# Perceiver block on one core: the two slot streams change the order of their half passes

## The chip, the cores and the metric

The kernel runs on one core of a Trainium2 chip. A core has TensorE (PE, matmuls; its weight loads are listed as PEld), VectorE (DVE), ScalarE (ACT), GpSimd (POOL) and SyncE (SP, here only a DMA queue), and 16 DMA engines. The metric is device time in microseconds (us) of one execution, lower is better. The kernel before took 1061.83 us (median of 3 runs, 1057.53 to 1068.19).

## The reference

`x` has 8 batches of 64 slots of width 512, `ctx_1024` has 8 batches of 1601 rows of width 512, all float32. Three blocks follow each other, each added to `x`. The first is the one that the change is in:

```python
Pn = rmsnorm(P, input_norm_w); k_proj = Pn @ Wk.T; v_proj = Pn @ Wv.T     # P = ctx_1024
for _ in range(3):
    sn = rmsnorm(slots, slot_norm_w); q_proj = sn @ Wq.T
    scores = einsum('bkd,bmd->bkm', q_proj, k_proj) * SCALE
    attn = softmax(scores, axis=-2)                        # over the 64 slots
    attn = attn / (sum(attn, axis=-1, keepdims=True) + EPS)
    updates = einsum('bkm,bmd->bkd', attn, v_proj)
    slots = gru_cell(updates, slots, wih, whh, bih, bhh)   # gates r, z, n
```

Then come a 16-head self-attention over 64 positions, and a mixture of 8 experts (2 per row) with 2 shared experts.

## The kernel before

**Tiling.** The 8 batches are four pairs, t = 0 to 3; a pair is 128 slots on 128 partitions. Its context has 13 row tiles of 128 rows per batch (the last has 65). `k_proj` and `v_proj` are never formed: `Wq` and `Wk` are folded into `wqk`, and `Wv` and the input gates' weights into `wvi` (`fold_values`, three parts of 32 matmul instructions), so both products run against the raw context.

**One pass** (t, it) has two halves, which the code calls X and Y.

- X is `attend`: transpose the slots (`tr_s`, copied to `sT`), query `pq` = `sT` x `wqk`, copy it (`q`), transpose it (`tr_q`), scale it (`qT`), score it in four column groups (`sc`, lines 358 to 370: 64 matmul instructions per pass) against the transposed context, copy each group into `raw` (ACT); then the softmax in four chunks of up to four tiles: transposes `tr_e`, then reduce, subtract, multiply, Exp, sum, reciprocal, two multiplies on DVE and ACT (lines 395 to 402, result `e`), and the weighted sums `part` on POOL (lines 404 to 410). In the first pass of a pair X also makes the transposed context (`prepare`): 26 tiles are transposed (`tr_p`), copied to `pT_a` by DVE and ACT in turns, squared on ACT for the norm, and written to DRAM (`kept`), from where later passes load it (`pT_X`).
- Y is `update`: `pu` = `e` x raw context rows (52 matmul instructions, line 433), `rs` (line 440), the recurrent part of the gates `recur` (`pr`, `pz`, `phn` <- `whh`, `sT`: 8 instructions each), `upd` = `pu` scaled (DVE, then ACT), transpose (`tr_u`, copied to `uT`), the input part of the gates (`pr`, `pz`, `pxn` <- `wvi`, `uT`: 8 each), and lines 456 to 470, which make the new slots on DVE and ACT.

**Order of the halves.** Pairs 0 and 2 are one stream (`lead`, six passes), pairs 1 and 3 the other (`trail`). The list `stages` (lines 199 to 204) gives X(0,0) Y(0,0), and then four halves at a time: X trail, X lead, Y trail, Y lead. So two X follow each other, and then two Y: X(1,0) X(0,1) Y(1,0) Y(0,1), X(1,1) X(0,2) Y(1,1) Y(0,2), X(1,2) X(2,0) Y(1,2) Y(2,0), X(3,0) X(2,1) Y(3,0) Y(2,1), X(3,1) X(2,2) Y(3,1) Y(2,2), X(3,2), and Y(3,2) at line 723, behind the first two pairs' projections of the self-attention. The loop at lines 504 to 521 issues them.

**What sets the order on an engine.** The framework's planner orders the instructions when the program is built: where they stand in the program is their priority, and an instruction that is not ready by its reckoning lets a later one of the same engine pass. In the trace, recurrent matmuls of one stream stand between the scores of the other. On the chip every engine then works its list in order. DMAs that are issued through `queue` keep the program's order on SP. `pump` (line 242) puts them there: `plan` lists, by stage, which row chunks (`nat`, 5 buffers of 1 MB) and transposed groups (`ctxT`, 5 buffers) are wanted, and each `done` frees a buffer and lets the next load be issued.

**PSUM.** There are 8 banks, four of the tag `gate` and four of the tag `ring`. `gate` holds `pr`, `pz`, `phn`, `pxn`, and `tr_p` of `prepare`; `ring` holds everything else. The buffer tag `wide` (`raw` and `e`) has 3 buffers, `sT`, `quT` and `nat` of the work pool have 2 each.

Of the kernel before, what the change touches and what calls it, by code (L numbers as in the profile page):

```python
# [39 lines left out]
def perceiver_kernel(  # L40
# [155 lines left out]

    lead = [(t, it) for t in (0, 2) for it in range(ITERS)]
    trail = [(t, it) for t in (1, 3) for it in range(ITERS)]  # L200
    stages = [("X", lead[0]), ("Y", lead[0])]
    for n in range(len(trail)):
        both = trail[n : n + 1] + lead[n + 1 : n + 2]
        stages += [("X", u) for u in both] + [("Y", u) for u in both]

# [62 lines left out]
    def prepare(t):  # L270

        ss = small.tile([P, NMT, 2], F32, tag="pss", name=f"pss_{t}", bufs=4)
        nc.gpsimd.memset(ss, 0.0)
        for g, (lo, hi) in enumerate(GROUPS):
            for j in range(2):
                b = 2 * t + j
                key = plan["ctxT"].pop(0)[1]
                assert key == ("made", "X", t, 0, j, g)
                held["ctxT"] += 1
                ct = chunk(f"pT_{b}_{g}_a", "ctxT")[:, : DC * (hi - lo)]  # L280
                c3 = ct.rearrange("p (c m) -> p c m", c=DC)
                for i in range(lo // P, (hi + P - 1) // P):
                    src = row_tile("X", t, 0, j, i)
                    k = src.shape[0]
                    junk = work.tile([P, D], F32, tag="junk", name=f"junk_{b}_{i}")
                    nc.scalar.activation(  # L286
                        junk[:k], src, AF.Square, accum_out=ss[:k, i, j : j + 1]
                    )
                    evacuate(
                        c3[:, :, i * P - lo : i * P - lo + k],  # L290
                        transpose4(src, f"p_{b}_{i}", k, "gate"),
                    )
                    row_used(i)
                nc.gpsimd.dma_start(kept[b][g], ct)  # L294
                tiles[key] = c3
            yield g
        v = small.tile([P, NMT, 2], F32, tag="pv", name=f"pv_{t}", bufs=2)
        nc.vector.tensor_scalar(v, ss, 1.0 / D, 1e-6, ALU.mult, ALU.add)
        ri = const.tile([P, NMT, 2], F32, name=f"inv_{t}")
        flat = "p i j -> p (i j)"  # L300
        rsqrt(ri.rearrange(flat), v.rearrange(flat), 2 * NMT, f"p_{t}")
        rms = const.tile([P, NMT, 2], F32, name=f"rms_{t}")
        nc.vector.tensor_mul(rms, v, ri)
        inv_of[t], rms_of[t] = ri, rms
# [27 lines left out]

    slots_of, sT_of = {}, {}

    def attend(t, it, first=lambda g: None):

        n = f"{t}_{it}"
        slots = slots_of[t]
        sT = work.tile([P, DC, P], F32, tag="sT", name=f"sT_{n}", bufs=2)
        nc.vector.tensor_copy(sT, transpose4(slots, f"s_{n}"))  # L340
        sT_of[t] = sT
        ss = small.tile([P, 1], F32, tag="sss", name=f"sss_{n}")
        junk = work.tile([P, D], F32, tag="junk", name=f"junk_{n}")
        nc.scalar.activation(junk, slots, AF.Square, accum_out=ss)
        nc.vector.tensor_scalar(ss, ss, 1.0 / D, 1e-6, ALU.mult, ALU.add)
        ri = small.tile([P, 1], F32, tag="sri", name=f"sri_{n}")

        pq = bank(f"pq_{n}")
        matmul4(pq, lambda c: sT[:, c, :], lambda c: wqk[:, c, :])
        q = work.tile([P, D], F32, tag="nat", name=f"q_{n}", bufs=2)  # L350
        nc.scalar.copy(q, pq)
        rsqrt(ri, ss, 1, f"s_{n}")
        qT = work.tile([P, DC, P], F32, tag="quT", name=f"qT_{n}", bufs=2)
        nc.vector.tensor_mul(  # L354
            qT, transpose4(q, f"q_{n}"), qscale.unsqueeze(2).to_broadcast([P, DC, P])
        )
        raw = work.tile([P, NMT * P], F32, tag="wide", name=f"raw_{n}", bufs=3)
        for g, (lo, hi) in enumerate(GROUPS):
            first(g)
            sc = bank(f"sc_{n}_{g}")[:, : hi - lo]  # L360
            cols = [tiles[("col" if it else "made", "X", t, it, j, g)] for j in range(2)]
            for c in range(DC):
                for j in range(2):
                    nc.tensor.matmul(  # L364
                        sc[j * S : (j + 1) * S, :],
                        lhsT=qT[:, c, ts(j, S)], rhs=cols[j][:, c, :],
                        start=c == 0, stop=c == DC - 1,
                    )
            done("ctxT", 2)
            nc.scalar.mul(raw[:, lo:hi], sc, ri)  # L370

        e = work.tile([P, NMT * P], F32, tag="wide", name=f"e_{n}", bufs=3)
        mx = small.tile([P, 2 * NMT], F32, tag="mx", name=f"mx_{n}")
        sm = small.tile([P, 2 * NMT], F32, tag="sm", name=f"sm_{n}")
        inv = inv_of[t].rearrange("p i j -> p (i j)")
        rms = rms_of[t].rearrange("p i j -> p (i j)")

        part = work.tile([P, P], F32, tag="part", name=f"part_{n}", bufs=2)
        for lo in range(0, NMT, 4):
            hi = min(lo + 4, NMT)  # L380
            k = P if lo < MT else TAIL
            pt = bank(f"tr_e_{n}_{lo}")[:k, : (hi - lo) * P]
            for i in range(lo, hi):
                nc.tensor.transpose(pt[:, ts(i - lo, P)], raw[:, i * P : i * P + k], ident)  # L384
            r, w = slice(2 * lo, 2 * hi), 2 * (hi - lo)

            def rows3(v):
                return v.rearrange("p (r k) -> p r k", k=S)

            def wide(v):  # L390
                return v[:k, r].unsqueeze(2).to_broadcast([k, w, S])

            ee = rows3(e[:k, lo * P : hi * P])
            mxr, smr = mx[:k, r], sm[:k, r]
            nc.vector.reduce_max(mxr, rows3(pt), axis=AX.X)  # L395
            nc.vector.tensor_sub(ee, rows3(pt), wide(mx))
            nc.vector.tensor_mul(ee, ee, wide(inv))  # L397
            nc.scalar.activation(ee, ee, AF.Exp)  # L398
            nc.vector.reduce_sum(smr, ee, axis=AX.X)
            nc.vector.reciprocal(smr, smr)  # L400
            nc.vector.tensor_mul(smr, smr, inv[:k, r])
            nc.vector.tensor_mul(ee, ee, wide(sm))
            prod = raw[:k, lo * P : hi * P]
            nc.gpsimd.tensor_mul(rows3(prod), ee, wide(rms))  # L404
            if hi - lo > 1:
                nc.gpsimd.tensor_add(prod[:, : 2 * P], prod[:, : 2 * P], prod[:, 2 * P :])
                one = part if lo == 0 else prod[:, :P]
                nc.gpsimd.tensor_add(one, prod[:, :P], prod[:, P : 2 * P])
            if lo:
                nc.gpsimd.tensor_add(part[:k], part[:k], prod[:, :P])  # L410
        return e.rearrange("p (i k) -> p i k", k=P), part

    def recur(t, it):

        n = f"{t}_{it}"
        banks = [bank(f"{g}_{n}", "gate") for g in ("pr", "pz", "phn", "pxn")]
        for j, pg in enumerate(banks[:3]):
            matmul4(
                pg, lambda c: sT_of[t][:, c, :], lambda c: whh_s[j][:, c, :], stop=j == 2
            )  # L420
        return banks

    def update(t, it, att, banks=None):

        n = f"{t}_{it}"
        e, part = att
# [19 lines left out]
        upd = work.tile([P, D], F32, tag="nat", name=f"upd_{n}", bufs=2)  # L446
        nc.vector.tensor_scalar_mul(upd[:, :H], pu[:, :H], cs)
        nc.scalar.mul(upd[:, H:], pu[:, H:], cs)
        uT = work.tile([P, DC, P], F32, tag="quT", name=f"uT_{n}", bufs=2)
        nc.vector.tensor_copy(uT, transpose4(upd, f"u_{n}"))  # L450
        for j, pg in enumerate((pr, pz, pxn)):
            matmul4(
                pg, lambda c: uT[:, c, :], lambda c: wvi[j][:, c, :], start=j == 2
# [21 lines left out]


    wvi = [chunk3(f"wvi_{j}") for j in range(3)]
    whh_s = []

    def fold_values(j):  # L480
        for dc in range(DC):
# [7 lines left out]
    def start_group(g):  # L489
# [2 lines left out]
            return  # L492
        for n in (g, g + 1):
            next(columns)
            if g == 0:
                fold_values(n)
        if g == 0:
            whh_s.extend(load_w(whhT, j, f"whh_{j}", queue) for j in range(2))
        if g:
            for _ in columns:  # L500
                pass

    att = {}
    for pos, (half, (t, it)) in enumerate(stages[:-1]):
        if pos == 1:
            fold_values(2)
            whh_s.append(load_w(whhT, 2, "whh_2", queue))
        if half == "Y":
            update(t, it, att.pop(t))
            continue  # L510
        if it == 0:
            slots_of[t] = work.tile([P, D], F32, tag="slots", name=f"slots_{t}_0", bufs=4)
# [1 line left out]
            columns = prepare(t)  # L514
            if pos == 0:
                done("nat", 2)
                att[t] = attend(t, it, start_group)
                continue
            for _ in columns:
                pass  # L520
        att[t] = attend(t, it)

# [520 lines left out]
```

## Time and profile before

| | |
|---|---|
| median of 3 runs | 1061.83 us |
| the profiled execution | 1067.05 us, span 1065.3 us, mean granted TensorE clock 0.969 |
| PE busy | 971.7 us, 91% of the span, 4081 matmul instructions |
| DVE, ACT, POOL busy | 428.6, 246.7, 198.0 us |
| DMA | 237.41 MB, mean 223 GB/s |
| slot passes (102 to 783 us of the span) | PE busy 634.03 of 681 us, DMA 247 GB/s |
| what follows (783 to 1065 us) | PE busy 247.35 of 282 us |

The page's slices are 26.6 us each, with the busy share in tenths. Matmuls are pipelined and their ends are modelled, so "busy" is not a statement that the array does useful work at its peak; the idle time in front of a matmul, which the timeline puts in brackets with what ended it, is what an order can remove. A float32 matmul of 512 columns is two instructions; eight in a row take 3.43 to 3.70 us. In the timeline a row `x8` is eight instructions, and the first number is their start.

### The profile page before, as it was taken

The numbers are of one execution on the slowest core, as the hardware profiler recorded it, in microseconds if no ns is written. First come the engines' busy times: TensorE is split into PE (matmuls) and PEld (weight loads), VectorE is DVE, ScalarE is ACT, GpSimd is POOL, SyncE is SP. The second block draws the span as 40 slices with busy tenths as digits, with TensorE's granted clock in tenths as the row PEclk, the third lists the DMA queues.
The fourth block names the chain that finished last, engine by engine and source line by source line (L and its number), as shares of the span: only waits on it lengthen the run. The fifth ranks groups of instructions, "written<-read, shape, count | busy, mean of one in ns | idle before, by whom it ended". The sixth has DMA issues, their size and how long they took to land. (4 is left out here: it accounts for less than half of the span.)

```text
span 1065.3 us, 11266 instructions
## 1 busy us (share of the span) xinstructions
PE 971.7 (91%) x4081; PEld 461.3 (43%) x4081; DVE 428.6 (40%) x1059; ACT 246.7 (23%) x530; POOL 198.0 (19%) x295
## 2 busy tenths in 40 slices
PE   6899989899989997999898899899998988899994
PEld 3454354334433444444543344333443464675441
DVE  3224155532544347522554224452451445542223
ACT  1652552110211524205521001110110111211220
POOL 2003013300133004300132100330051211031221
PEclk9999999999999998999899999999999969999998
DMA  9946678864656647845787564596191300039943
GB/s 344 400 135 274 249 296 347 317 255 168 246 232 263 246 136 270 316 151 214 306 336 270 223 247 186 197 357 247 59 348 40 129 2 0 1 134 309 371 158 136
DMA packets 62425, 237.41 MB, mean 223 GB/s; under 512 B 5870, under 2 KB 20222, under 8 KB 50080
## 3 DMA queue, kind: packets, MB, share of 16 engines
q1 hardware_dynamic: 52576, 195.44, 48.6%
q0 software_dynamic: 8640, 39.14, 9.4%
q10 hardware_dynamic: 1152, 2.10, 0.5%
q8 instruction: 33, 0.54, 0.2%
q14 instruction: 24, 0.20, 0.0%
HBM read 201.22 MB, written 36.48 MB: 223 GB/s over the span
## 5 line engine op out<-in xcount | busy, mean ns | idle before, releaser
L433 PE MATMUL pu<-pn_Y,e 128*64 128x512 f32 x576 | 144.1, 609 | 5.7 <-DMA pn_Y<-in_ctxp 5.7
L364 PE MATMUL sc<-pT_X,qT 128*64 128x384 f32 (+1 forms) x512 | 102.4, 505 | 11.7 <-DMA pT_X<-kept 7.4
L404 POOL TENSOR_TENSOR raw<-e,rms 128x512 f32<-128x512 f32 (+1 forms) x48 | 44.8, 936 | 275.4 <-DVE sm L400 153.1
L433 PEld LDWEIGHTS pu<-pn_Y,e 128*64 128x64 f32 x576 | 42.3, 139 | 95.7 <-issue 79.6
L286 ACT ACTIVATE junk<-pn_X 128x512 f32<-128x512 f32 x96 | 60.4, 629 | 40.9 <-DMA pn_X<-in_ctxp 38.6
L364 PEld LDWEIGHTS sc<-pT_X,qT 128*64 128x64 f32 x512 | 38.1, 136 | 70.2 <-issue 47.8
L110 PE MATMUL tr_p<-ident,pn_X 128*128 128x128 f32 x384 | 53.4, 290 | 14.0 <-DMA pn_X<-in_ctxp 8.8
L395 DVE TENSOR_REDUCE mx<-tr_e 128x8 f32<-128x512 f32 (+1 forms) x48 | 26.9, 581 | 97.4 <-PE tr_e L384 97.3
L294 POOL DMA_DIRECT2D kept<-pT_a x32 | 17.4, 545 | 214.3 <-ACT r L467 66.3
L84 DVE COPY pT_a<-tr_p 128x512 f32<-128x512 f32 x52 | 34.7, 685 | 53.1 <-PE tr_p L110 31.8
L110 PEld LDWEIGHTS tr_p<-ident,pn_X 128*128 128x128 f32 x384 | 44.4, 147 | 26.9 <-issue 14.6
L370 ACT ACTIVATE raw<-sc,sri 128x384 f32<-128x384 f32 (+1 forms) x48 | 28.6, 596 | 107.8 <-PE sc L364 107.6
L153 PE MATMUL pq<-wqk,sT 128*128 128x512 f32 x96 | 48.0, 646 | 4.9 <-DVE sT L340 3.9
L153 PE MATMUL pr<-wvi,uT 128*128 128x512 f32 x96 | 45.5, 617 | 4.1 <-DVE uT L450 3.9
L398 ACT ACTIVATE e<-e 128x512 f32<-128x512 f32 (+1 forms) x48 | 25.8, 547 | 98.9 <-DVE e L397 98.8
L364 PE MATMUL sc<-pT_a,qT 128*64 128x384 f32 (+1 forms) x256 | 46.2, 503 | 2.4 <-DVE qT L354 2.4
L153 PE MATMUL pr<-whh,sT 128*128 128x512 f32 x96 | 48.1, 612 | 0.0
L153 PE MATMUL pqkv<-wqkv,haT 128*128 128x512 f32 x96 | 44.2, 618 | 1.4 <-ACT haT L549 1.4
L153 PE MATMUL pz<-whh,sT 128*128 128x512 f32 x96 | 44.7, 597 | 0.0
L153 PE MATMUL pab<-up_b,xT 128*128 128x512 f32 x96 | 43.2, 594 | 0.8 <-ACT xT L86 0.7
L153 PE MATMUL phn<-whh,sT 128*128 128x512 f32 x96 | 43.5, 592 | 0.0
L153 PE MATMUL pz<-wvi,uT 128*128 128x512 f32 x96 | 43.2, 592 | 0.0
(240 smaller groups left out, 1348.1 us busy)
## 6 DMA issues: line engine op xcount, KB each, us to landing
pn_Y<-in_ctxp SPq DMA_DIRECT2D x72, 1024.0 KB
pT_X<-kept SPq DMA_DIRECT2D x48, 768.0 KB
pn_X<-in_ctxp SPq DMA_DIRECT2D x24, 1024.0 KB
kept<-pT_a POOLq DMA_DIRECT2D x24, 768.0 KB, 8.6
pT_X<-kept SPq DMA_DIRECT2D x16, 898.0 KB
up_b<-in_w SPq DMA_DIRECT2D x24, 512.0 KB
kept<-pT_a POOLq DMA_DIRECT2D x8, 898.0 KB, 10.1
dn_b<-in_w SPq DMA_DIRECT2D x12, 512.0 KB
```

What stands on the lines that cost most here:

```text
L84: nc.vector.tensor_copy(dst, src)
L110: nc.tensor.transpose(pt[:, c, :rows], src[:rows, ts(c, P)], ident[:rows, :rows])
L153: nc.tensor.matmul(dst, lhsT=lhsT(c), rhs=rhs(c), start=start and c == 0, stop=stop and c == DC - 1,)
L286: nc.scalar.activation(junk[:k], src, AF.Square, accum_out=ss[:k, i, j : j + 1])
L294: nc.gpsimd.dma_start(kept[b][g], ct)
L364: nc.tensor.matmul(sc[j * S : (j + 1) * S, :], lhsT=qT[:, c, ts(j, S)], rhs=cols[j][:, c, :], start=c == 0, stop=c == DC - 1,)
L370: nc.scalar.mul(raw[:, lo:hi], sc, ri)
L395: nc.vector.reduce_max(mxr, rows3(pt), axis=AX.X)
L398: nc.scalar.activation(ee, ee, AF.Exp)
L404: nc.gpsimd.tensor_mul(rows3(prod), ee, wide(rms))
L433: nc.tensor.matmul(pu[j * S : (j + 1) * S, :], lhsT=e[:k, i, ts(j, S)], rhs=row_tile("Y", t, it, j, i), start=i == 0, stop=i == MT,)
```

## The change

The list of halves is now X(0,0) X(1,0) Y(0,0), and then X lead, Y trail, X trail, Y lead in turns, and Y(3,2) at the end as before. Each X is followed by the Y of the other stream. Three things go with it:

- An X with it > 0 first issues `recur` of the pair whose Y comes next, in two parts: gates r and n (js = 0, 2) ahead of `attend`, gate z behind `pq`. That Y is then given these banks and doesn't issue `recur` itself. Y behind an X with it = 0, and Y(3,2), issue `recur` as before.
- The softmax of tiles 8 to 11 and of tile 12 isn't issued in X but in the Y that follows it: the one between `upd` and `tr_u`, the other between `uT` and the input gates. (X(0,0), which an X follows, issues them at its end.)
- Every X with it = 0 issues `prepare` by groups between its scores, as X(0,0) did before; for pairs 1 to 3 `tr_p` takes banks of `ring` and not of `gate`.

```diff
-    stages = [("X", lead[0]), ("Y", lead[0])]
-    for n in range(len(trail)):
-        both = trail[n : n + 1] + lead[n + 1 : n + 2]
-        stages += [("X", u) for u in both] + [("Y", u) for u in both]
+    stages = [("X", lead[0]), ("X", trail[0]), ("Y", lead[0])]
+    for n in range(1, len(lead)):
+        stages += [("X", lead[n]), ("Y", trail[n - 1]), ("X", trail[n]), ("Y", lead[n])]
+    stages.append(("Y", trail[-1]))
...
-                        transpose4(src, f"p_{b}_{i}", k, "gate"),
+                        transpose4(src, f"p_{b}_{i}", k, "ring" if t else "gate"),
...
-    def attend(t, it, first=lambda g: None):
+    def attend(t, it, first=lambda g: None, behind_q=lambda: None):
...
         matmul4(pq, lambda c: sT[:, c, :], lambda c: wqk[:, c, :])
+        behind_q()
...
-        for lo in range(0, NMT, 4):
+        def softmax(lo):
...
-        return e.rearrange("p (i k) -> p i k", k=P), part
-
-    def recur(t, it):
+
+        for lo in (0, 4):
+            softmax(lo)
+        late = [lambda: softmax(8), lambda: softmax(12)]
+        return (e.rearrange("p (i k) -> p i k", k=P), part), late
+
+    def recur(t, it, js=(0, 1, 2), banks=None):
...
-        banks = [bank(f"{g}_{n}", "gate") for g in ("pr", "pz", "phn", "pxn")]
-        for j, pg in enumerate(banks[:3]):
+        if banks is None:
+            banks = [bank(f"{g}_{n}", "gate") for g in ("pr", "pz", "phn", "pxn")]
+        for j in js:
...
-    def update(t, it, att, banks=None):
+    def update(t, it, att, banks=None, late=()):
...
         nc.scalar.mul(upd[:, H:], pu[:, H:], cs)
+
+        for part_of_it in late[:1]:
+            part_of_it()
         uT = work.tile([P, DC, P], F32, tag="quT", name=f"uT_{n}", bufs=2)
         nc.vector.tensor_copy(uT, transpose4(upd, f"u_{n}"))
+        for part_of_it in late[1:]:
+            part_of_it()
...
         if half == "Y":
-            update(t, it, att.pop(t))
+            update(t, it, att.pop(t), begun.pop((t, it), None), late)
+            late = ()
             continue
...
-                att[t] = attend(t, it, start_group)
-                continue
-            for _ in columns:
-                pass
-        att[t] = attend(t, it)
+            att[t], late = attend(t, it, start_group)
+            if stages[pos + 1][0] == "X":
+                for part_of_it in late:
+                    part_of_it()
+                late = ()
+            continue
+
+        other = stages[pos + 1][1]
+        begun[other] = recur(*other, (0, 2))
+        att[t], late = attend(t, it, behind_q=lambda: recur(*other, (1,), begun[other]))
```

In `start_group` the folds of the weights and the loads of `whh` are now done only for the first pair (`not wvi_done`); the third fold and the load of `whh_2` still stand ahead of the second entry of `stages`, which is now X(1,0).

## The prediction

> **What bounds the kernel now.** I read the page's busy shares and slices first, then the busy time by stretch, then PE's idle time stage by stage in the timeline.
>
> ```profile
> PE 971.7 (91%) x4081; PEld 461.3 (43%) x4081; DVE 428.6 (40%) x1059; ACT 246.7 (23%) x530; POOL 198.0 (19%) x295
> ...
> PE   6899989899989997999898899899998988899994
> ...
> PEclk9999999999999998999899999999999969999998
> ```
>
> PE is the busiest engine by far, in nearly every slice. The next view, busy time by stretch (window, its length, PE, PEld, DVE, ACT, POOL, granted clock, DMA share, GB/s), gives what an order can win.
>
> ```profile
> 102.00:783.00 681.00, 634.03 (x2514) 279.15 (x2514) 287.65 (x700) 164.37 (x359) 116.62 (x160) 0.98 0.64 247
> 404.00:421.00 17.00, 11.73 (x36) 6.08 (x36) 13.16 (x44) 8.93 (x25) 10.80 (x16) 0.70 0.90 336
> 521.00:528.00 7.00, 5.54 (x14) 2.13 (x12) 0.79 (x3) 4.12 (x12) 0.00 (x0) 0.78 1.01 426
> ```
>
> In the slot passes PE is idle for 681 - 634 = 47 us. The change adds and removes no instruction, so 47 us is the whole stake, with what the lower clock costs there. PE's timeline shows where it lies. First a half X with other work beside it, X(1,1):
>
> ```profile
> 270.29 6.02 PE L364 MATMUL sc<-pT_X,qT 128*64 128x384 f32 x34
> 276.24 1.12 PE L153 MATMUL pr<-whh,sT 128*128 128x512 f32 x2
> 277.43 2.79 PE L364 MATMUL sc<-pT_X,qT 128*64 128x384 f32 x14
> 280.15 1.12 PE L153 MATMUL pr<-whh,sT 128*128 128x512 f32 x2
> ```
>
> The waits for the next column group are filled with the other stream's recurrent gates: idle 0.0 us. Then the X that follows it, X(0,2), with those gates used up, and the Y behind it:
>
> ```profile
> 298.82 0.66 PE L110 MATMUL tr_q<-ident,q 128*128 128x128 f32 x4 [0.73 <-ACT q L351]
> 300.26 6.02 PE L364 MATMUL sc<-pT_X,qT 128*64 128x384 f32 x34 [0.78 <-DVE qT L354]
> 307.46 3.22 PE L364 MATMUL sc<-pT_X,qT 128*64 128x384 f32 x16 [1.18 <-DMA pT_X<-kept]
> ...
> 316.04 0.66 PE L384 MATMUL tr_e<-ident,raw 128*128 128x128 f32 x4 [0.73 <-ACT raw L370]
> ...
> 331.14 0.41 PE L110 MATMUL tr_u<-ident,upd 128*128 128x128 f32 x2 [1.06 <-DVE upd L447]
> 331.47 1.07 PE L433 MATMUL pu<-pn_Y,e 128*64 128x512 f32 x2
> ```
>
> Every link of X's chain is bare here. Adding the brackets over all stages (X and Y with pair and pass):
> - first X of a couple: (1,1) 0, (1,2) 0.8, (3,1) 0, (3,2) 0.8; second X: (0,1) 4.1, (0,2) 3.7, (2,1) 4.9, (2,2) 4.0. Eight X with it > 0: 18.3 us.
> - the eleven Y: 13.2 us (0.9 + 2.3 + 2.3 + 0.9 + 4.4 + 2.3 by couples), of it 1.06 us per couple at `tr_u`, 0.5 to 0.9 at the `uT` copy, 0.7 (once 2.9) for row chunks.
> - X(1,0), X(2,0), X(3,0), which prepare a pair: 4.7 + 6.3 + 4.2 = 15.1 us.
>
> The sum, 46.6, is the 47 of the window. Of it 16.7 us end with a DMA, the rest with DVE or ACT. In X(2,0) there is more to see:
>
> ```profile
> 405.01 0.66 PE L110 MATMUL tr_p<-ident,pn_X 128*128 128x128 f32 x4 [1.25 <-ACT pT_a L86]
> ...
> 409.87 1.12 PE L110 MATMUL tr_p<-ident,pn_X 128*128 128x128 f32 x4 [1.58 <-DVE pT_a L84]
> ...
> 413.78 5.88 PE L153 MATMUL pq<-wqk,sT 128*128 128x512 f32 x8
> ```
>
> Four transposes of 0.66 us take 1.12 us, and `pq` 5.88 us where its other passes take 3.70: the granted clock was 0.70 here. Such excess, against the same group at full clock: here 3 x 0.46 + 2.18 = 3.6 us, `pq` at 520 (5.55) 1.85, `pu` at 589 (4.57 against 3.22) 1.35: 6.8 us. So at most 46.6 + 6.8 = 53 us can go.
>
> On this clock the Trainium skill speaks against my sum: "TensorE: Matmul & The Clock Gate" (The HAM clock gate) says that the clock falls to half after an idle window of about 3.4 us. No gap of the slot passes is that long, so by the page nothing would be lost or won, and the sum below would be 23 us instead of 28. The row shows 0.70 where the longest single gap was 1.58 us; the measurement decides.
>
> **The change, part by part.**
>
> *Turns of X and Y, gates ahead of X.* X(trail, n) now follows Y(trail, n-1), so new slots, transpose, `sT` and `pq` are a bare chain of one stream. Its length: last `pxn` ends at 231.2, the new slots at 234.87 + 0.69 = 235.6, that is 4.4 us; `tr_s` 0.6; the `sT` copy with its hand-over 1.2 (the wait in X(0,1)): 6.2 us. Ahead of it stand gates r and n, 16 instructions or 2 x 3.43 = 6.9 us, whose inputs are an X old. Their banks come free early: `pr` is read (L460) 3 us before `pxn` starts, `phn` needs no `pxn`. So that chain is covered, barely. Gate z (3.43 us) covers the `q` copy (0.73). If the cover failed, each of 8 X would pay up to 6 us.
>
> What is late next in X is `qT` (0.78) and the transposed groups: with 5 `ctxT` buffers the sixth and later tiles are still loaded while X scores (1.0 to 1.7 us bare). The gates are used up by then; what can fill is `pu` of the other stream, whose `e` is done and whose first five row chunks were loaded in the Y before. I take 1.0 us per X, nearer to the filled X (0 to 0.8) than to the bare one (3.7 to 4.9), since the 0.73 at `tr_e` goes in any case with the late softmax. 18.3 - 8 = gain 10.3 us; ends 0 (all bare at 4) and 18.3.
>
> *Softmax tiles 8 to 12 in the other Y.* Their transposes (4 + 1, 0.5 us) stand in the `upd` and `uT` waits, and beyond them `pu` of the next Y can fill, as the row at 331.47 shows. Eleven Y at 0.5 us: 13.2 - 5.5 = gain 7.7; ends 0 and 13.2. But their DVE work is now ahead of the `uT` copy: reduce 0.58, subtract 0.68, multiply 0.68 = 1.94 us (mean durations). DVE takes its list in order, and `uT`, then the input gates, then the new slots queue behind. Bare that would cost 11 x 1.94 = 21 us; filled by `pu`, 0. I take 0.5 each: cost 5.5. `e` itself is wanted one half later than before, so the late tiles make no Y late. The three `wide` buffers suffice (`raw` and `e` of one stream, `e` of the other).
>
> *Preparation.* With `tr_p` out of the `gate` banks and the Y behind not begun, that Y's whole `recur` (24 instructions, 10.3 us) can fill X(1,0), X(2,0), X(3,0). I take 1.5 us left in each: gain 15.1 - 4.5 = 10.6; ends: a loss, priced as rival C, and 15.1. The scores between the column groups change little: the trace before already has them so (5 `ctxT` buffers force it).
>
> *Loads.* The bytes are the same. Requests on SP now alternate 8 `ctxT` and 6 row chunks, where before 16 and 12 came together; a `ctxT` load waits for its buffer in front of row loads, but both are wanted a half later. In an X that prepares, 6.6 MB of `kept` go out and the next Y's 6.6 MB come in: 13.1 MB at the 426 GB/s of the row at 521 are 31 us, against some 28 us of PE work there plus 10.3 of `recur`. In the same place before (X(2,0), then Y(1,2) at 439) `pu` didn't wait. I take 0; ends -5 and +5. "DMA: Bandwidth & Descriptors" (Where 436 GB/s comes from) of the Trainium skill puts a core's HBM limit near 358 GB/s, which would make it 37 us, still within the 38; the row shows more than that limit.
>
> *Clock.* With gaps gone I take back 5 of the 6.8 us; ends 0 and 6.8.
>
> *Start and end.* The first 102 us and everything from 783 on keep their work; Y(2,2) now stands between X(3,2) and the projections, which gives the loads of `wqkv` time. 0, ends -3 and +3.
>
> **Sum.** 10.3 + 7.7 - 5.5 + 10.6 + 5 = 28 us. The profiled execution, 1067.05, would become 1039; it lies 5 us above the median of the runs shown, from which 1061.83 - 28 = **1034 us**.
>
> **The rivals.**
>
> A, *everything is filled*: only the 1.0 us `ctxT` waits or so stay. For it: X(1,1) and X(3,1) have 0.0 us idle. Against: each stage has a link that the planner reckons shorter than it is. 46.6 - 6 + 6.8 = 47 us: 1014 us.
>
> B, *the wait changes its place*: the planner already filled what it saw, and what is left are hand-overs of 0.7 us that it doesn't see; they stay, and 1.94 us of DVE work ahead of `uT` is added. For it: bare `qT`, `uT` and `upd` waits stand in the trace though `pu` work was there. Half of the gain, 14 to 17 us, against half to all of the 21 us: 1056 to 1064, say 1060. The change would then not do what it says.
>
> C, *slower: `ring` is crowded where a pair is prepared*. `tr_p` now shares four banks with `pq`, `tr_q`, `sc`, `tr_e`, and with a `pu` that was begun early and holds its bank through the whole X. Each tile's copy waits on DVE and ACT behind softmax and squares. For it: in the stretch 405 to 413 six tiles cost 4.8 us of idle, 0.8 per tile, and the clock fell. Against: at 135.5 to 142.2 fifteen tiles went through four banks at full rate. If half of the 78 tiles of pairs 1 to 3 go at that pace, 31 us, with 3.6 us of clock in each of three stages, 11 us, less the 10.3 + 7.7 won elsewhere: +24, or 1086 us. It decides from about 25 slow tiles on.
>
> **How the numbers follow.** The forecast 0.50 (1022 to 1048 with its middle bounds), A 0.15, B 0.18, C 0.17. Faster by over 1% (under 1051; a measurement of this kernel, 1057 to 1068, can't tell less) is the forecast, A and a little of B: 0.67. Within 1%: 0.16. Slower by over 1%: C, 0.17. The range goes from 1014 (A) to 1066 (B), and leaves out C and what lies below A.
>
> **What would show it.** Right: PE idle in the slot passes near 20 us; recurrent gates ahead of `tr_s` and behind `pq`; `pu` of the other stream between column groups; no 0.73 at `tr_e`; granted clock near 1 at the preparations. Wrong: waits at `pr` for `uT` of 1 to 2 us in every Y (B); `tr_p` waiting for `pT_a` in three stages (C); `pq` waiting for `sT` in every X (the 6.9 us cover fails); `pu` waiting for row chunks behind a preparation. The step that I trust least is that `pu` fills what the gates no longer fill.

## The result: slower by 3.9%

The changed kernel takes 1104.58 us (median, 1100.77 to 1106.76) against 1062.92 us for the kernel before (1057.53 to 1068.19): a ratio of 1.0388, with a 95% interval of 1.0328 to 1.0449. The forecast was 1034, with a range up to 1066. Even the rival on the slower side, C at 1086, falls short, and it named another mechanism.

First the page of the changed kernel, its busy shares and the slices of PE and of the DMA rate:

```profile
PE 970.8 (88%) x4081; PEld 476.6 (43%) x4081; DVE 415.8 (38%) x1059; ACT 242.1 (22%) x530; POOL 186.3 (17%) x295
...
PE   6999979889797989898889798979999988899994
...
PEclk9999989999899999899989899999999989999998
...
GB/s 344 390 153 229 345 416 98 274 203 191 286 92 385 8 297 161 411 173 228 416 214 155 322 39 379 59 309 168 100 384 147 136 28 1 1 73 327 372 164 134
```

PE's work is the same, 970.8 us against 971.7. The span grew by 37.5 us, from 1065.3 to 1102.8, and PE's idle time by 38.4, from 93.6 to 132.0: all of the loss is idle time of PE. The DMA row shows a new pattern, 416 then 98, 385 then 8, 411 then 173: the DMA engines work in bursts, with pauses between.

The busy time by stretch has the slot passes (now 102 to 826 us) and what follows:

```profile
102.00:826.00 724.00, 636.21 (x2509) 296.99 (x2507) 277.94 (x691) 149.18 (x325) 118.31 (x179) 0.96 0.59 234
826.00:1102.00 276.00, 245.15 (x1249) 134.09 (x1248) 103.44 (x265) 41.71 (x79) 54.76 (x87) 0.95 0.40 140
```

The idle time of the slot passes is 724 - 636 = 88 us where it was 47. What comes after them is 6 us shorter than before (282). The view of who waits for whom, PE alone and in the slot passes alone (total us, times, longest), says what ends these 88 us:

```profile
PE pu L443 <- DMA pn_Y<-in_ctxp: 44.7, 14, 7.2
PE pr L153 <- DVE uT L463: 12.2, 11, 1.2
PE sc L368 <- DMA pT_X<-kept: 8.8, 8, 1.2
PE tr_p L110 <- ACT raw L374: 7.5, 5, 1.9
PE sc L368 <- DVE qT L358: 6.3, 8, 0.8
PE tr_u L110 <- DVE upd L457: 5.6, 10, 0.6
```

The same view of the kernel before, for its slot passes:

```profile
PE sc L364 <- DMA pT_X<-kept: 7.4, 9, 1.7
PE sc L364 <- DVE qT L354: 6.5, 8, 0.9
PE pu L433 <- DMA pn_Y<-in_ctxp: 5.0, 4, 2.9
...
PE tr_u L110 <- DVE upd L447: 4.2, 4, 1.1
PE pr L153 <- DVE uT L450: 3.9, 6, 0.9
PE pq L153 <- DVE sT L340: 3.9, 4, 1.2
```

One wait is nearly the whole loss: `pu` waits 44.7 us for row chunks, where it waited 5.0, and that is 39.7 of the 41 us. Next to it the `uT` wait rose by 8 us; the `sT` wait is gone, as the change meant it.

One half X and the Y behind it, X(0,1) and Y(1,0), in PE's timeline of the changed kernel:

```profile
197.03 6.02 PE L368 MATMUL sc<-pT_X,qT 128*64 128x384 f32 x34 [0.79 <-DVE qT L358]
204.23 3.22 PE L368 MATMUL sc<-pT_X,qT 128*64 128x384 f32 x16 [1.19 <-DMA pT_X<-kept]
...
208.41 1.50 PE L443 MATMUL pu<-pn_Y,e 128*64 128x512 f32 x5
...
212.34 6.27 PE L443 MATMUL pu<-pn_Y,e 128*64 128x512 f32 x28
221.93 3.22 PE L443 MATMUL pu<-pn_Y,e 128*64 128x512 f32 x13 [3.33 <-DMA pn_Y<-in_ctxp]
...
227.81 0.41 PE L110 MATMUL tr_u<-ident,upd 128*128 128x128 f32 x2 [0.56 <-DVE upd L457]
```

`pu` does 34 of its 52 instructions, which use up four of the five chunks in the buffers and the first tile of the fifth, and waits for the sixth. SP's queue in the same stretch tells what stands in front of that chunk:

```profile
199.85 13.57 SPq L118 DMA_DIRECT2D pT_X<-kept  x8
214.35 11.59 SPq L118 DMA_DIRECT2D pn_Y<-in_ctxp  x6
```

Eight group loads, three for this X and five (3.9 MB) for the *next* X, whose scores begin at 257.56, were requested from 199.85 to 213.4; the first of the six row chunks at 214.35, once the first chunk's buffer was free. It is used at 221.93, 7.6 us after its request. In the kernel before, the chunk requested at 320.31 was used at 325.26, 4.95 us after. The request itself isn't late here: it follows the start of the row of 28 `pu` instructions by 2.0 us (212.34 to 214.35), as it does in e1_defer below (205.09 to 207.10). How busy the DMA is around it (last two columns: DMA share, GB/s):

```profile
205.00:213.00 8.00, 8.00 (x46) 4.21 (x44) 4.75 (x8) 2.05 (x4) 0.00 (x0) 1.00 1.01 408
213.00:222.00 9.00, 5.67 (x29) 2.64 (x27) 1.86 (x7) 0.32 (x1) 5.08 (x7) 1.00 0.97 380
222.00:230.00 8.00, 6.28 (x30) 2.51 (x30) 3.03 (x8) 0.47 (x1) 0.00 (x0) 1.00 1.01 419
230.00:257.00 27.00, 26.78 (x64) 11.94 (x64) 11.86 (x34) 4.04 (x8) 3.44 (x6) 0.94 0.16 61
```

From 205 to 230 the DMA is full, and then for 27 us, in which PE works through the gates and frees no buffer, it moves 61 GB/s.

The trace has a comparison of its own. Eight Y follow an X with it > 0. In two of them no next X needs groups loaded: Y(0,2), since X(2,0) makes its own, and Y(2,2), the last in the loop. Their row waits, at 403.12 and 803.30:

```profile
403.12 3.22 PE L443 MATMUL pu<-pn_Y,e 128*64 128x512 f32 x13 [0.44 <-DMA pn_Y<-in_ctxp]
...
803.30 3.22 PE L443 MATMUL pu<-pn_Y,e 128*64 128x512 f32 x13 [0.62 <-DMA pn_Y<-in_ctxp]
```

The six others wait 3.33, 5.15, 3.81, 5.29, 4.48 and 4.76, 26.8 us in all; the three Y behind a preparation wait 16.8 us. With the 1.06 above that is the 44.7.

So theory Q: **the sixth row chunk comes late because the groups for the next X are ahead of it in a DMA stream that is full just then.** From the start of the scores to the landing of that chunk it takes 24.9 us here (197.03 to 221.93) and 25.0 us before (300.26 to 325.26). That the two are alike shows little by itself: before, the chunk was requested 20.1 us after the start of the scores and was there 4.95 us later; here it is requested after 17.3 us and takes 7.6. Before, PE came to that chunk after 24.3 us; the change took work and waits out of the X, so that PE comes after 21.6 us and waits for the rest. Rival B2: there are five row buffers, the sixth chunk can't be requested earlier, and what else is in flight doesn't matter.

### The profile page after: what moved, and what is told of

Read it like the earlier page. It is cut to its first block, busy times and chain, and to the rows that moved or that the text cites. A ratio compares the mean times of both kernels' runs of the same rounds, so it can differ in the third digit from the quotient of the medians.

```text
span 1102.8 us, 11300 instructions
## 1 busy us (share of the span) xinstructions
PE 970.8 (88%) x4081; PEld 476.6 (43%) x4081; DVE 415.8 (38%) x1059; ACT 242.1 (22%) x530; POOL 186.3 (17%) x295
## 5 line engine op out<-in xcount | busy, mean ns | idle before, releaser
L443 PE MATMUL pu<-pn_Y,e 128*64 128x512 f32 x576 | 155.8, 650 | 44.7 <-DMA pn_Y<-in_ctxp 44.7
L443 PEld LDWEIGHTS pu<-pn_Y,e 128*64 128x64 f32 x576 | 54.6, 148 | 133.2 <-issue 73.3
L368 PEld LDWEIGHTS sc<-pT_X,qT 128*64 128x64 f32 x512 | 42.4, 136 | 64.2 <-issue 36.3
L153 PE MATMUL pr<-wvi,uT 128*128 128x512 f32 x96 | 51.7, 688 | 12.4 <-DVE uT L463 12.4
L110 PEld LDWEIGHTS tr_p<-ident,pn_X 128*128 128x128 f32 x384 | 47.2, 153 | 23.1 <-ACT raw L374 9.1
L458 ACT ACTIVATE upd<-pu,cs 128x256 f32<-128x256 f32 x12 | 5.7, 474 | 198.2 <-DVE upd L457 198.2
L153 PE MATMUL pr<-whh,sT 128*128 128x512 f32 x96 | 44.7, 594 | 0.0
L153 PE MATMUL pq<-wqk,sT 128*128 128x512 f32 x96 | 43.3, 594 | 1.1 <-ACT pT_a L86 1.0
L153 PE MATMUL pxn<-wvi,uT 128*128 128x512 f32 x96 | 43.2, 592 | 0.0
```

The source lines that it names most:

```text
L110: nc.tensor.transpose(pt[:, c, :rows], src[:rows, ts(c, P)], ident[:rows, :rows])
L153: nc.tensor.matmul(dst, lhsT=lhsT(c), rhs=rhs(c), start=start and c == 0, stop=stop and c == DC - 1,)
L368: nc.tensor.matmul(sc[j * S : (j + 1) * S, :], lhsT=qT[:, c, ts(j, S)], rhs=cols[j][:, c, :], start=c == 0, stop=c == DC - 1,)
L443: nc.tensor.matmul(pu[j * S : (j + 1) * S, :], lhsT=e[:k, i, ts(j, S)], rhs=row_tile("Y", t, it, j, i), start=i == 0, stop=i == MT,)
```

## The experiments

All ran beside the kernel before, whose median over their groups was 1060 to 1062 us; ratios are to it.

**e1_defer.** One condition in `pump`:

```diff
                 if q and q[0][1][0] != "made" and held[tag] < BUFS[tag]
+                and not (tag == "ctxT" and plan["nat"] and plan["nat"][0][0] < q[0][0])
```

> The changed kernel, but a transposed group isn't requested while row chunks that are wanted by an earlier half are still to be requested: the five groups for the next X are queued behind the last row chunk of the Y between. Theory Q (the last row chunk of each Y arrives late because the groups for the next X, 4 MB, are ahead of it in the DMA stream): PE's wait of pu for row chunks falls from 44.7 to under 12 us, and the clock loss behind these waits goes too: 1055 to 1070 us. Rival B (five row buffers: the sixth chunk can't be requested before the first is used up, whatever else is in flight): wait and time stay, 1098 to 1107 us.

Measured: 1058.88 us, ratio 0.9991 (0.9958 to 1.0025). The row wait fell to 15.8 us. The same place in SP's queue and in PE's timeline:

```profile
192.68 2.90 SPq L118 DMA_DIRECT2D pT_X<-kept  x3
207.10 0.33 SPq L118 DMA_DIRECT2D pn_Y<-in_ctxp  x1
207.48 2.72 SPq L118 DMA_DIRECT2D pT_X<-kept  x5
```

```profile
205.09 6.27 PE L444 MATMUL pu<-pn_Y,e 128*64 128x512 f32 x28
212.02 3.22 PE L444 MATMUL pu<-pn_Y,e 128*64 128x512 f32 x13 [0.67 <-DMA pn_Y<-in_ctxp]
```

The chunk is now requested ahead of the five groups, and is used 4.9 us later; the Y behind an X with it > 0 wait 0.6 to 0.9 us. The time lies in the forecast of theory Q, the wait a little above its 12 us: 10.2 us of it stay at the three Y behind a preparation, where there were 16.8. In two of these the changed kernel's request is late as well: in Y(0,0) it comes at 151.10, behind four group requests and 12.8 us after `pu` began (138.27); here it comes 3.7 us after (137.07 to 140.74). What stays there is a full DMA: it moves 419 GB/s from 128 to 160 us, with no pause. Rival B2 is out: the buffers are the same, the request comes as long after `pu` began, and the chunk is there sooner. And the `sc` wait for groups stayed at 9.4 us, so the groups come early enough.

**e9_dose2.** The same condition, with `held[tag] >= 2` added to what is held back: two of the five groups may go ahead.

> The changed kernel with a partial hold: of the five groups for the next X, two may be requested ahead of the last row chunk of the Y between (all five in the changed kernel, none in e1_defer). Theory Q goes by the bytes that stand in front: pu's wait for row chunks, 44.7 us with five and 15.8 with none, lies between, at 20 to 32 us, and the time at 1068 to 1085 us. If only the hold as such counts (the order of requests on SP, not the bytes): at one of the two ends, 1056 to 1062 or 1100 to 1107.

Measured: 1066.48 us, ratio 1.0019 (0.9984 to 1.0054); row wait 17.7 us. A miss: the wait with two groups is nearly what it is with none, which is what the second forecast said, and the time lies in neither range. The trace shows why the two groups cost little: they were requested by 202.5, the chunk at 210.10, and just ahead of that the DMA had almost nothing left to move (last row: share 0.15, 59 GB/s).

```profile
195.56 6.94 SPq L118 DMA_DIRECT2D pT_X<-kept  x5
210.10 0.33 SPq L118 DMA_DIRECT2D pn_Y<-in_ctxp  x1
215.28 3.22 PE L447 MATMUL pu<-pn_Y,e 128*64 128x512 f32 x13 [0.92 <-DMA pn_Y<-in_ctxp]
207.00:210.00 3.00, 3.00 (x18) 1.78 (x16) 2.83 (x9) 1.79 (x3) 0.00 (x0) 1.00 0.15 59
```

So what counts is not how many bytes were requested ahead, but what the DMA hasn't finished when the chunk is requested; in the changed kernel its share at that point was 0.97 to 1.01. The price begins somewhere between two groups and five.

**e8_before_defer.** The condition in the kernel before.

> The kernel before with the same hold on the group loads. Theory Q: where two Y follow two X, pu waits 5.7 us in all for row chunks, so there is little to win, and the groups for the next X still have a whole Y: 1055 to 1063 us, no difference. If the hold is a gain in itself, apart from the new order: 1020 to 1045.

Measured: 1062.64 us, ratio 1.0019 (0.9993 to 1.0045). No difference: the hold is no gain in itself, it repairs what the new order breaks.

**e10_order_alone.** The changed kernel with `recur` wholly in its own Y and all four softmax chunks in X:

```diff
-        begun[other] = recur(*other, (0, 2))
-        att[t], late = attend(t, it, behind_q=lambda: recur(*other, (1,), begun[other]))
+        att[t], late = attend(t, it)
...
-        for lo in (0, 4):
+        for lo in (0, 4, 8, 12):
             softmax(lo)
-        late = [lambda: softmax(8), lambda: softmax(12)]
+        late = []
```

> The changed kernel without its early gates and without its late softmax: the order of the halves alone, with the preparation between the scores and its transposes in ring. Theory Q says that the order alone already brings most of the loss in the row wait, since each Y now stands right behind an X whose freed buffers are refilled first; the gates in their own Y fill a part: 1070 to 1085 us. If the order alone isn't at fault, but only gates and softmax: 1045 to 1060 us.

Measured: 1086.57 us, ratio 1.0247 (1.0181 to 1.0314). The time is 1.6 us above the forecast of theory Q. The order alone brings more than half of the loss; the row wait is 26.5 us, of it 16.3 in two Y behind a preparation (8.8 and 7.5), while Y(1,0), Y(0,1), Y(1,1) and Y(0,2) wait 0.5 to 0.7. The gates and the softmax are back between their scores, and PE comes to the sixth chunk later. The six Y with groups ahead wait 8.4 us in all, where the changed kernel has 26.8: there the order alone is not enough.

**e3_nobegun**, only the first part of that diff, and **e2_nolate**, only the second.

> The changed kernel, but recur stays wholly in its own Y, as before the change. Theory Q: the recurrent gates can then stand in the wait for the last row chunk, or in the X chain, wherever the planner sees room; the row wait of 44.7 us falls to 10 to 30: 1070 to 1095 us. If the place of the gates doesn't matter to that wait: 1100 to 1110, with bare waits for sT in X on top.

> The changed kernel with all four softmax chunks issued in X, none in the following Y. If the late softmax is what delays the uT copy (PE waits 12.2 us at the input gates for uT against 3.9 before), that wait falls to about 4 us and the 0.73 us at tr_e in X comes back, but lies within the wait for the row chunk (theory Q): 1092 to 1098 us. If the uT wait has another cause: 1101 to 1107 us.

Measured: without the early gates 1074.90 us, ratio 1.0115 (1.0049 to 1.0182), row wait 23.9 us, and the waits of `sc` for `qT` and for groups (15.1 us) are gone but for 1.0 us. Without the late softmax 1090.73 us, ratio 1.0263 (1.0190 to 1.0336). This second edit gained more than expected, and not where I expected it: the `uT` wait fell only from 12.4 to 9.1 us, and the `upd` wait rose from 6.6 to 11.6; it is the row wait that fell, from 44.7 to 22.4. In the six Y with groups ahead either edit takes most of the wait away: 26.8 us become 5.7 without the early gates and 4.4 without the late softmax. In Y(1,0) the ways differ. Without the late softmax PE comes to the chunk later, when the DMA has nearly caught up (share 0.89 from the request on), and the chunk, requested at 217.61, is used 5.0 us after. Without the early gates it still takes 7.0 us (213.21 to 220.21), but four instructions of gate n stand in the wait. So it takes all three, the order, the early gates and the late softmax, to make these waits as long as they are.

**e4_gate.** `tr_p` back in the `gate` banks.

> The changed kernel with the context transposes of pairs 1 to 3 in the gate banks as before. If sharing the ring banks costs time (rival C of the prediction; in the trace after, tr_p waits 7.5 us for ACT copies of raw), it gains 5 to 8 us: 1096 to 1100. If not, the recurrent gates can no longer run beside the preparation: 1103 to 1112 us.

Measured: 1092.65 us, ratio 1.0305 (1.0233 to 1.0377). It gains 12 us, more than expected; but `tr_p` waits as long as before the edit (7.8 us, now for `pT_a`), and what fell is the row wait, to 33.7. The fall lies at the three Y behind a preparation, 16.8 to 6.3 us; the six with groups ahead wait 25.9, as before the edit. The timelines suggest why, though no run isolates it: in Y(0,0) all 24 recurrent instructions now stand in the row wait (145.57 to 156), while with `tr_p` in `ring` ten of them ran ahead of `pu`, between the steps of the preparation, and 14 were left for it.

**Towards a better kernel.** The rest builds on e1_defer.

**e5_defer_lateuT**: both late chunks behind the `uT` copy.

```diff
-        for part_of_it in late[:1]:
-            part_of_it()
         uT = work.tile([P, DC, P], F32, tag="quT", name=f"uT_{n}", bufs=2)
         nc.vector.tensor_copy(uT, transpose4(upd, f"u_{n}"))
-        for part_of_it in late[1:]:
+        for part_of_it in late:
             part_of_it()
```

> As e1_defer, and the late softmax chunks (tiles 8 to 11, and 12) are both issued behind the uT copy instead of the first ahead of it. If the DVE work of that chunk ahead of the copy makes the uT wait (12.0 us in e1_defer, 1.16 per Y), it falls to about 5 us, while the 0.44 us of transposes no longer stand in the upd wait (5.5 rises to about 10): 1053 to 1058 us. If the copy is late for another reason: 1057 to 1061.

Measured: 1046.94 to 1054.84 us in three of its four runs, ratio 0.9892 (0.9828 to 0.9956); the fourth took 1974.50 us and isn't in the ratio. The `uT` wait fell to 4.6 us and the `upd` wait rose to 9.5, as expected. DVE's timeline of the changed kernel shows the cause, the late softmax's reduce and subtract between `upd` and the copy:

```profile
227.18 0.48 DVE L457 TENSOR_SCALAR upd<-pu,cs 128x256 f32<-128x256 f32 x1
227.58 1.08 DVE L399 TENSOR_REDUCE mx<-tr_e 128x8 f32<-128x512 f32 x2
228.58 0.68 DVE L400 TENSOR_TENSOR e<-tr_e,mx 128x512 f32<-128x512 f32 x1
229.18 0.68 DVE L463 COPY uT<-tr_u 128x512 f32<-128x512 f32 x1
```

**e6_defer_phn**: besides, gate n isn't issued in X but in its own Y, behind the `uT` copy (`begun[other] = recur(*other, (0,))` in X, and `recur(t, it, (2,), (pr, pz, phn, pxn))` in `update`). **e7_defer_nobegun**: e1_defer with `recur` wholly in its own Y.

> As e5_defer_lateuT, and of the recurrent gates of the next Y only r and z are issued in X (r ahead of attend, z behind pq); gate n (8 instructions, 3.43 us) is left to its own Y, where it is the filler with the lowest rank. If what is left of PE's waits in X (qT 0.78, column groups 1.1) and at the last row chunk (0.7) only lacks ready work, gate n fills them: 2.5 us in each of 8 X/Y couples: 1030 to 1042 us, faster than the kernel before. If the waits are no shorter with ready work beside them (the instruction that waits stands first in PE's list): 1050 to 1060.

> e1_defer and e3_nobegun together: groups held back, and recur wholly in its own Y. In e3_nobegun the waits of sc for qT and for groups are gone and pu still waits 23.9 us for row chunks. Theory Q: the hold takes 12 to 16 us of these: 1052 to 1062 us. If in e3_nobegun the rows are late for another reason than the groups in front: 1070 to 1076.

Measured: 1039.53 us, ratio 0.9785 (0.9746 to 0.9823), and 1037.71 us, ratio 0.9772 (0.9719 to 0.9826). Both beat the kernel before, and e7 beat its expectation. PE's timeline of e7_defer_nobegun, an X and its Y:

```profile
241.06 6.02 PE L369 MATMUL sc<-pT_X,qT 128*64 128x384 f32 x34
247.01 1.13 PE L153 MATMUL phn<-whh,sT 128*128 128x512 f32 x2
248.15 2.79 PE L369 MATMUL sc<-pT_X,qT 128*64 128x384 f32 x14
...
257.79 6.27 PE L444 MATMUL pu<-pn_Y,e 128*64 128x512 f32 x28
263.98 1.12 PE L153 MATMUL phn<-whh,sT 128*128 128x512 f32 x2
265.04 3.22 PE L444 MATMUL pu<-pn_Y,e 128*64 128x512 f32 x13
```

No bracket is left on these lines: with the lowest rank, the planner puts gate n, two instructions at a time, into the waits for a group and for the sixth row chunk. Issued early, as the change does it, gates r and n stand in one block of 16 ahead of `tr_s`. In e7 ten instructions (`pr` and two of `pz`, from 229.17) cover that place with no wait at `tr_s`, and the rest is left for the other waits.

**e11_defer_nobegun_lateuT**: e7 with e5's edit.

> e7_defer_nobegun with both late softmax chunks behind the uT copy, as in e5_defer_lateuT. If the gain there (uT wait 12.0 to 4.6 us) adds to e7: 1030 to 1035 us. If the recurrent gates already filled that place in e7 and the upd wait is bare now: 1036 to 1041 us.

Measured: 1032.96 us (1030.20 to 1034.88), ratio 0.9715 (0.9673 to 0.9756), the fastest kernel of the study. Its slot passes:

```profile
102.00:760.00 658.00, 628.56 (x2529) 287.00 (x2528) 278.28 (x695) 149.18 (x326) 124.48 (x184) 1.00 0.66 261
```

658 - 629 = 29 us of idle time where the kernel before had 47 and the changed kernel 88, and a granted clock of 1.00.

## Why the prediction was wrong

*The stake* held: PE bounds, and the whole difference is PE's idle time, though its sign was the other.

*The step that failed* is "Loads": "I take 0; ends -5 and +5". It measured 39.7 us (44.7 - 5.0). I compared the bytes of a preparation with the DMA's rate, and took "both are wanted a half later" for an answer. I had not set the freed buffers against time: in an X right in front of a Y, eight groups and six chunks are requested within 26 us, the refill for the next X goes out first, and the DMA is full for just this stretch and empty in the next. I saw the order on SP and gave it no price. e1_defer shows this cause, by time and by trace, for 28.9 of the 44.7 us: at the six Y with groups ahead 26.8 us become 4.0, behind a preparation 16.8 become 10.2. The 10.2 belong to the same step: I had set 31 us of bytes against 38 us of PE work and found room, but in e1_defer the DMA is full around all three places (417 to 420 GB/s) and `pu` waits. I didn't take apart which bytes my sum left out. "`pu` waiting for row chunks behind a preparation" stood among my signs of being wrong, but without a price.

*The X chain* was right in its mechanism. The `sT` wait went from 3.9 to 0 us, as 6.9 us of gates against a chain of 6.2 said (e7 shows that less is enough), and the `tr_e` wait is gone. The size was wrong: I took 1.0 us left per X, 8 of 18.3 us, and `sc` waits 15.1 us over eight X, 1.9 each. "`pu` fills what the gates no longer fill", the step that I trusted least, didn't hold for `qT` and the third group: the gates had been the filler there. e7_defer_nobegun, which leaves them to the planner, has neither wait, but for 0.9 us at the groups.

*The late softmax*: forecast 5.5 us left and 5.5 us of cost, 11; measured 12.2 + 5.6 = 17.8. DVE work ahead of `uT` was the right mechanism, though of the 1.94 us only the reduce and the subtract stand ahead of the copy, and rival B held a part of it; nothing filled it. e5_defer_lateuT takes 7.4 us of the `uT` wait away, and adds 4.0 to the `upd` wait.

*The preparation*: forecast 4.5 us left, measured about 10 (`tr_p` 7.5 for `raw` and 1.3 for `qT`, `tr_q` 1.3). The loss at `tr_p` that rival C priced at 31 us didn't come: its waits are no longer than before.

*The clock*: forecast 5 us back. Instead seven `pu` groups behind a row wait take 4.9 to 5.7 us in place of 3.22, 14 us in all (one such group, 1.35, before). In e1_defer five of the seven are back at 3.22, and PE's busy time is 960.2 us, 10.6 less. Against the kernel before, the changed kernel's busy time didn't rise, so something else in it became shorter; I didn't isolate it. "TensorE: Matmul & The Clock Gate" (The HAM clock gate) of the Trainium skill asks for an idle window of about 3.4 us; these waits are 3.8 to 7.2 us long, and the one of 3.33 us left its group at 3.22, which agrees. Other rows don't: behind a wait of 2.32 us in e1_defer and of 2.59 in e10_order_alone the same group took 4.92 and 4.91, and the trace before has 0.70 behind gaps of up to 1.58.

*Start and end*: 0 forecast, within 3; the end won 6 us, outside these ends.

Without the row wait, what remains is 88 - 45 = 43 us of other idle time, against 42 without it before (47 - 5): no gain either. e1_defer says the same with 0.9991. So three things were wrong, the loads, the filler and the place of the late softmax: with the first two mended the kernel gains 2.3% (e7), with all three 2.85% (e11, 28.9 us). That this is near the 28 us of my forecast is chance, not a confirmation: e11 issues no gates early, and its gain has other terms. What I didn't settle: where the price of the groups in front begins, between two and five, and which of the bytes around a preparation make the waits that stay.

## What to carry to other kernels

When an order is changed, draw up for each buffer when it is freed and what the freed space requests, in the new order: two consumers side by side free two sets of buffers at once, and in one queue the load that is wanted last can stand in front of the one that is wanted next. Request loads in the order in which they are wanted, not in the order in which buffers come free. And independent work that already fills gaps is a stock: issuing it early in a block spends it, and the gaps that it filled come back (e5 to e6: eight instructions left to the planner, 14 us).

## What the runs showed of the hardware

- The DMA moved 408, 380 and 419 GB/s in three stretches one after the other at a share near 1.0 (205 to 230 us), loading alone. "DMA: Bandwidth & Descriptors" (Where 436 GB/s comes from) of the Trainium skill puts the HBM limit of a core near 358; the measurement is above it. With the writes of a preparation among the loads it moved 419 as well (e1_defer, 128 to 160 us). A chunk of 1 MB was used 4.9 us after its request with little ahead of it and 7.6 us with the groups ahead.
- The clock also fell without a long gap. In e1_defer the input gates took 5.40 us in place of 3.70 in Y(0,1) (from 276.39 us), where the gaps of the last 8 us were 0.69, 0.56 and 1.15; in Y(1,0), with nearly the same gaps (0.67, 0.56 and 1.16), they took 3.70. The granted clock was 0.72 in the first (276 to 282 us) and 1.00 in the second (220 to 224).
